# A third row tile for one key and one value tile, and a new timetable for the row work, in an attention block with norms and feed-forward on one Trainium2 core

## The chip, the cores and the metric

The kernel runs on one core of one Trainium2 chip. The metric is the device time of one execution in microseconds (us), the median of three runs. All arithmetic is in float32 apart from the stored mask.

## The reference

There are F = 8 graphs ("frames") of N = 2048 rows with C = 256 channels, H = 8 heads of D = 32, and one adjacency matrix for all of them. Cut to what matters:

```python
qkv = einsum('fnc,ck->fnk', x, w_qkv);  q, k, v = split(qkv, 3)      # heads of 32
scores = einsum('fnhd,fmhd->fhnm', q, k) / sqrt(32)
scores = where(adj > 0, scores, -1e9)
t = einsum('fhnm,fmhd->fnhd', softmax(scores), v)
a = layernorm(x + t) * ln1_g + ln1_b
h = relu(a @ w1 + b1)
b = layernorm(a + h @ w2 + b2) * ln2_g + ln2_b
out = layernorm(x + b)
```

So each row has one softmax attention over 2048 keys, then three norms: after the attention, after the feed-forward, and of the sum with x.

## The kernel before

**Items.** Rows go in chunks of 512 (`CH`), four of them a frame (`NCK`). The eight heads go in two groups `g` of four. Keys go in 16 blocks `mb` of 128. An item is (f, qc, g, mb): frame, chunk of query rows, group of heads, key block. There are 1024 items, 128 to a frame (`FRAME`), 32 to a chunk, and one pass of the main loop (one step) for each. A step `t` issues, in this order: side work (`advance(t)`), the exponentials of item t+1, the scores of item t+2, the values of item t, and the sums of item t.

- `scores` (L230, TensorE): four products key by query, one for each head, into two PSUM tiles of 128x1024. VectorE adds the mask on the way out into a `p` tile of 1 MB (L233, two adds).
- `exponentials` (L237, ScalarE): in place over the `p` tile.
- `values` (L249, TensorE): four products `p` by v, summed in PSUM over the 16 items of a group. At the last one ScalarE copies the sum to `oT` (L253).
- `add_up`: the denominators need the sum of the 16 `p` tiles of a group. Seven blocks (`POOLED` = 0, 3, 6, 8, 11, 13, 15) are added by GpSimd into block 0 (L271, `p<-p` of 128x2048). Eight others form two chains (`MOVED` = 1, 4, 7, 10 and 2, 5, 9, 12) that are summed by accumulating DMAs out of GpSimd's queue (L268, 1 MB each, also `p<-p`). Block 14 stays alone. Each transfer of a chain waits for the one before it.
- A generator `denominator` sums the four remaining tiles with a product by ones (L315); the last of the four terms is asked for four steps after the group's end (`SUM` = 4). ScalarE copies the result to `dT` (L317), TensorE transposes it, and VectorE takes the reciprocal and two running checks (L326 to L328).

There are 12 `p` tiles, which block t+2 takes in turn.

**A chunk's row work.** When both groups of a chunk have their denominators, `outcome` runs: `divide` transposes each `oT` and multiplies by the reciprocals (L353, VectorE) into a row tile `y`; a DMA out of GpSimd's queue adds x (L339, 512 KB). Then a generator `tail` does the rest:

- `norm`: statistics of four 128x256 blocks on VectorE (L278, L279), `per` blocks in a step; then four small GpSimd instructions (L283 to L287) that end in `nb`; after a pause, four ScalarE activations (L290).
- `feed_forward`: transposes into `turned` (L456, ScalarE copy L457), two GpSimd instructions over the row tile (L459, L461), the first product into `hT` (L54 with `w1s`, L470), and after a pause the second product (L54 with `w2s`), which VectorE adds to the row tile (L483).
- a second `norm`, two GpSimd instructions (L363, L365), a DMA out of GpSimd's queue that adds x again (L367), a pause, a third `norm`, and the store out of SP's queue (L370).

There are two `y` tiles, and `ROOM` lets two tails be open at once. The last chunk of all has a path of its own (`finish`, `half_rows`), in which two halves of the rows take turns.

**What sets the order.** [...] Side work sits in generators in a list with a first step and a due step each. At each step `advance` resumes those whose step has come; `yield n` means "go on n steps later", `yield BANK` asks for a PSUM bank, of which one new user is let in at a step, and `yield MORE` continues a product in parts. Side products are paid out of a credit of 2200 a step (`STEP`) against 2048 for a product of 512 columns, and a due generator may go on without credit. `TURNED`, `ROOM` and `INPUTS` hold a generator until a shared tile is free.

`NEXT` says at which step of a frame the next frame's work starts: `turn` (transposes of x, kept in DRAM as `xd`), `ask` (queries, `wqkv`) and `project` (keys and values of chunk c and group g, `wqkv`; reads its transposed rows back through SP's queue, L196, and copies the results with L189 and L215). The keys and values of a frame are 8 + 8 tiles; the pools `kp` and `vp` hold 11 each, so a frame's projections reuse tiles of the frame that is still running. SP's queue carries the masks (L151, eight a chunk), these reloads and the stores.

GpSimd's queue (POOL) carries in order: L271, the issue of L268, L339 and L367, the four instructions to `nb`, L363, L365, L459 and L461.

Of the kernel before, what the change touches and what calls it, by code (L numbers as in the profile page):

```python
# [29 lines left out]
BANK, MORE, WAIT, TURNED, ROOM, INPUTS = -1, -2, -3, -4, -5, -10  # L30
# [31 lines left out]
def fast_path(ctx, tc, cst, x, adj, out, RS):  # L62
    nc = tc.nc
    F, N, C = x.shape
    NCK, TPC, MB = N // CH, CH // P, N // P
# [2 lines left out]
    dp = ctx.enter_context(tc.tile_pool(name="dp", bufs=1, space=bass.MemoryType.DRAM))  # L68
    mkp = ctx.enter_context(tc.tile_pool(name="mkp", bufs=MB // 2 + 1))
    ld = ctx.enter_context(tc.tile_pool(name="ld", bufs=LD))  # L70
    kp = ctx.enter_context(tc.tile_pool(name="kp", bufs=3 * NCK - 1))
    qp = ctx.enter_context(tc.tile_pool(name="qp", bufs=4))
    vp = ctx.enter_context(tc.tile_pool(name="vp", bufs=3 * NCK - 1))
    pp = ctx.enter_context(tc.tile_pool(name="pp", bufs=12))
    work = ctx.enter_context(tc.tile_pool(name="work", bufs=1))
    yp = ctx.enter_context(tc.tile_pool(name="yp", bufs=2))
    op = ctx.enter_context(tc.tile_pool(name="op", bufs=1))
    small = ctx.enter_context(tc.tile_pool(name="small", bufs=4))

# [6 lines left out]
    state = {"pair": 0, "side": None, "turn": 0, "turned": False, "holder": None, "tails": 0, "credit": 0}  # L86

    def columns(out, lhsT, rhs, start, stop):
        state["credit"] -= 4 * out.shape[-1]
        in_columns(nc, out, lhsT, rhs, start, stop)  # L90

    def transposes(ps, src, ident=ident):
        state["credit"] -= TURN
        for j, s in enumerate(src):
            nc.tensor.transpose(ps[:, j * P:(j + 1) * P], s, ident)  # L95
# [178 lines left out]
    def norm(t, per=1):  # L274
        mv = small.tile([P, TPC, nc.vector.BN_AGGR_DIM], F32, name="mv")
        for j in range(TPC):
            st = small.tile([P, nc.vector.BN_STATS_DIM], F32, name="st")
            nc.vector.bn_stats(st, t[:, j, :])  # L278
            nc.vector.bn_aggr(mv[:, j, :], st)  # L279
            if j % per == per - 1:  # L280
                yield 1
        rs = small.tile([P, TPC], F32, name="rs")
        nc.gpsimd.tensor_scalar(rs, mv[:, :, 1], EPS, 1.0, op0=ALU.add, op1=ALU.mult)  # L283
        nc.gpsimd.tensor_tensor(rs, rs, cst["mhalf"], ALU.pow)  # L284
        nb = small.tile([P, TPC], F32, name="nb")
        nc.gpsimd.tensor_tensor(nb, mv[:, :, 0], rs, ALU.mult)
        nc.gpsimd.tensor_scalar(nb, nb, -1.0, 1.0, op0=ALU.mult, op1=ALU.mult)  # L287
        yield 2
        for j in range(TPC):
            nc.scalar.activation(t[:, j, :], t[:, j, :], AF.Identity, bias=nb[:, j:j + 1], scale=rs[:, j:j + 1])  # L290
            if j % per == per - 1:
                yield 1

    def rows(v):
        return v[:, None, :].to_broadcast([P, TPC, C])
# [37 lines left out]
    def outcome(f, qc):  # L333
        yield ROOM
        state["tails"] += 1
        xin = x[f, qc * CH:(qc + 1) * CH, :].rearrange("(p j) c -> p j c", p=P)
        y = yp.tile([P, TPC, C], F32, name="y")
        yield from divide(f, qc, y)
        nc.gpsimd.dma_start(y, xin, accum_op=ALU.add)  # L339
        begin = items.index((f, qc, 1, LAST)) + SUM + 2  # L340
        if (f, qc) == (F - 1, NCK - 2):
            start(begin + 5, tail(f, qc, y, xin, 2), begin + 8)
        else:
            start(begin + 10, tail(f, qc, y, xin), begin + 26)

    def divide(f, qc, y):
        rc = RC.pop((f, qc))
# [9 lines left out]
    def tail(f, qc, y, xin, per=1):  # L357
        yield from norm(y, per)
        yield from feed_forward(y)
        yield 1  # L360
        z = y
        yield from norm(z, per)
        nc.gpsimd.tensor_tensor(z, z, rows(cst["g2r"]), ALU.mult)  # L363
        yield 1
        nc.gpsimd.tensor_tensor(z, z, rows(cst["be2r"]), ALU.add)  # L365
        yield 1
        nc.gpsimd.dma_start(z, xin, accum_op=ALU.add)  # L367
        yield 7
        yield from norm(z, per)
        nc.sync.dma_start(out[f, qc * CH:(qc + 1) * CH, :].rearrange("(p j) c -> p j c", p=P), z)  # L370
        state["tails"] -= 1
# [65 lines left out]
    def finish(f, qc):  # L437
        y = yp.tile([P, TPC, C], F32, name="y")
        xr, xb = state["rows"]
        yield from divide(f, qc, y)  # L440
        yT, hT = (work.tile([P, 2, CH], F32, name=n) for n in ("turned", "hT"))
        dst = out[f, qc * CH:(qc + 1) * CH, :].rearrange("(p j) c -> p j c", p=P)
        both = [half_rows(h, y, xr, xb, yT, hT, dst) for h in range(2)]
        while both:
            for e in list(both):
                if next(e, both) is both:
                    both.remove(e)

    def feed_forward(y):
        yield TURNED  # L450
        state["turned"] = True
        yT = work.tile([P, 2, CH], F32, name="turned")
        for a in range(2):
            yield BANK
            ps = bank()
            transposes(ps, [y[:, j, a * P:(a + 1) * P] for j in range(TPC)])  # L456
            nc.scalar.activation(yT[:, a, :], ps, AF.Identity, bias=cst["be1c"][:, a:a + 1], scale=cst["g1c"][:, a:a + 1])  # L457
        yield 1
        nc.gpsimd.tensor_tensor(y, y, rows(cst["g1r"]), ALU.mult)  # L459
        yield 1  # L460
        nc.gpsimd.tensor_tensor(y, y, rows(cst["be1b2r"]), ALU.add)  # L461
        hT = work.tile([P, 2, CH], F32, name="hT")
        for d in range(2):
            yield BANK
            ps = bank()
            for a in range(2):
                if a:
                    yield MORE
                columns(ps, w1s[:, a, d * P:(d + 1) * P], yT[:, a, :], start=(a == 0), stop=(a == 1))
            nc.scalar.activation(hT[:, d, :], ps, AF.Relu, bias=cst["b1s"][:, d:d + 1], scale=1.0)  # L470
        state["turned"] = False
        yield 1
        z = y
        for jj in range(0, TPC, 2):
            yield BANK
            ps = bank()
            for j in range(jj, jj + 2):
                if j > jj:
                    yield MORE
                for d in range(2):  # L480
                    columns(ps[:, (j - jj) * C:(j - jj + 1) * C], hT[:, d, j * P:(j + 1) * P], w2s[:, d, :],
                            start=(d == 0), stop=(d == 1))
            nc.vector.tensor_tensor(z[:, jj:jj + 2, :], ps.rearrange("p (b c) -> p b c", c=C), z[:, jj:jj + 2, :], ALU.add)  # L483
# [4 lines left out]
    def start(t, gen, due):  # L488
        fill.append([t, gen, 1, due])
        fill.sort(key=lambda e: e[3])  # L490
# [13 lines left out]
    def advance(t, finish=False):  # L504
        state["credit"] = min(max(state["credit"], 0) + STEP, KEPT)
        state["now"] = t
        free = not state["holder"]

        def more():
            if state["holder"] and state["holder"][2] == WAIT:  # L510
                return False
            due = [e[3] for e in fill if e[2] == BANK and e[0] <= t or e is state["holder"]]
            return finish or state["credit"] >= UNIT or min(due) <= t

        if state["holder"]:
            resume(state["holder"], t)
            while state["holder"] and more():
                resume(state["holder"], t)
        inputs = True
        for e in list(fill):  # L520
            while e[2] is not None and e[0] <= t and e is not state["holder"]:
                if e[2] == BANK:
                    if not free or not more():
                        break
                    free = False
                elif e[2] < INPUTS:
                    inputs = inputs and not any(u is not None for u in live[:INPUTS - e[2]])
                    if not inputs:
                        break
                elif e[2] == TURNED and state["turned"] or e[2] == ROOM and state["tails"] == 2:  # L530
                    break
                resume(e, t)
            while e is state["holder"] and more():
                resume(e, t)
# [6 lines left out]
    def ask(f, c):  # L541
# [2 lines left out]
        give(xT)  # L544

    NEXT = {1: [(turn, 0)], 2: [(ask, 1)], 20: [(turn, 1)], 34: [(ask, 2)], 40: [(project, 0, 0)], 50: [(turn, 2)],
            60: [(project, 1, 0)], 66: [(ask, 3)], 72: [(turn, 3)], 80: [(project, 2, 0)], 98: [(ask, 0)], 100: [(project, 3, 0)],
            104: [(project, 0, 1)], 108: [(project, 1, 1)], 112: [(project, 2, 1)], 116: [(project, 3, 1)]}

    def begin():  # L550
        todo = deque((qc, c) for qc in range(NCK) for c in range(NCK))
# [319 lines left out]
```

## Time and profile before

| | before |
|---|---|
| median of 3 runs | 3245.36 us (3242.5 to 3246.28) |
| profiled execution: time / span | 3246.02 us / 3244.1 us |
| PE (TensorE matmul) busy | 3109.4 us, 96% |
| DVE (VectorE) busy | 2735.7 us, 84% |
| ACT (ScalarE) busy | 2435.8 us, 75% |
| POOL (GpSimd) busy | 2592.2 us, 80% |
| mean granted TensorE clock | 0.985 |
| DMA | 590.52 MB, mean 182 GB/s; GpSimd's own queue (software) 66.9% of 16 engines' span |

How to read it. The profile is of one execution; its span is the time from its first to its last instruction. Busy time is that of data instructions; a matmul's end is modelled, so 96% on PE does not say that PE ran at its peak. PEld is the weight load, which overlaps PE. A group line gives line, engine, operation, output<-input, tile shapes, how often, then busy time and mean ns of one, then the idle time of the engine ahead of these instructions and what ended most of it. A line for DMA issues gives output<-input, queue, count, KB each and the median us from issue to landing. In a timeline a line gives start (us), duration, engine, source line, operation, output<-input, and in brackets the wait before it and what ended it ("issue" where the profile shows no other cause). Line numbers are those of the kernel before.

### The profile page before, as it was taken

The page shows a single profiled execution, that of the slowest core. Times are in us where ns is not written, and L with a number is a line of the kernel's source. Part 1 is how long each engine was busy: PE and PEld are TensorE (multiplying, and loading weights), DVE is VectorE, ACT ScalarE, POOL GpSimd, SP SyncE. Part 2 cuts the span into 40 slices and gives each one's busy share as a digit, 9 for nine tenths or more (in the row PEclk, how much of TensorE's full clock was granted, in tenths as well). Part 3 has the DMA queues.
Part 4 walks back from the last instruction along what each step waited for, and adds up shares of the span by engine and source line. Part 5 has one row for each costly group of instructions (what it writes and reads, how often), then busy time and mean ns, then how long its engine had stood idle before and what let it go on. Part 6 is the DMA issues. An engine that isn't in the chain of part 4 may idle for free.

```text
span 3244.1 us, 68406 instructions
## 1 busy us (share of the span) xinstructions
PE 3109.4 (96%) x28996; PEld 979.0 (30%) x28996; DVE 2735.7 (84%) x3203; ACT 2435.8 (75%) x1941; POOL 2592.2 (80%) x1358
## 2 busy tenths in 40 slices
PE   7899999999999999999999999999999999998985
PEld 4222333223332233322233323323233323332222
DVE  4888888888888888888988888888888888888975
ACT  3667778777777777778777778777778777777774
POOL 0568888888878888788887888888888788878884
PEclk8899999999999999999999999999999999999998
DMA  9688779778879788788787879878788878877763
GB/s 320 145 181 185 183 176 199 178 177 196 181 176 207 171 188 193 159 195 200 178 181 174 185 174 221 177 167 198 173 192 197 177 168 198 181 171 161 166 145 86
DMA packets 153240, 590.52 MB, mean 182 GB/s; under 512 B 15040, under 2 KB 67776, under 8 KB 103904
## 3 DMA queue, kind: packets, MB, share of 16 engines
q0 software_dynamic: 64416, 434.80, 66.9%
q1 hardware_dynamic: 87696, 149.98, 13.1%
q8 instruction: 229, 3.75, 0.4%
q10 hardware_dynamic: 816, 1.31, 0.1%
q14 instruction: 83, 0.68, 0.1%
HBM read 146.67 MB, written 37.75 MB: 57 GB/s over the span
## 4 chain that ended last, share of the span: by engine, by line
PE 75%; DVE 7%; POOL 5%; issue 4%; DMA 4%; ACT 2%; DVEq 0%; POOLq 0%; ACTq 0%
PE s L230 27%; PE x L249 24%; PE x L54 14%; PE x L315 6%; DVE p L233 6%; PE x L95 4%; DMA p<-p 3%; POOL p L271 2%; ACT p L237 1%; DMA mask<-md 1%; POOL y L365 1%; DVE st L278 1%; POOL y L363 0%; POOL y L461 0%; POOL y L459 0%
## 5 line engine op out<-in xcount | busy, mean ns | idle before, releaser
L233 DVE TENSOR_TENSOR p<-s,mask 128x1024 f32<-128x1024 f32 x2048 | 2409.3, 1218 | 372.7 <-PE s L230 209.9
L237 ACT ACTIVATE p<-p 128x2048 f32<-128x2048 f32 x1024 | 1956.1, 1910 | 521.4 <-DVE p L233 465.6
L271 POOL TENSOR_TENSOR p<-p 128x2048 f32<-128x2048 f32 x381 | 1825.5, 4793 | 223.7 <-ACT p L237 221.3
L230 PE MATMUL s<-qT,kT 32*128 32x512 f32 x8192 | 1173.8, 643 | 40.8 <-DVE p L233 35.9
L249 PE MATMUL x<-p,v 128*32 128x512 f32 x8192 | 1096.0, 607 | 16.7 <-ACT p L237 16.4
L268 POOL DMA_DIRECT2D p<-p x383 | 359.3, 956 | 306.9 <-ACT p L237 88.3
L230 PEld LDWEIGHTS s<-qT,kT 32*128 32x128 f32 x8192 | 321.1, 183 | 644.7 <-DVE p L233 587.2
L249 PEld LDWEIGHTS x<-p,v 128*32 128x32 f32 x8192 | 161.6, 108 | 797.8 <-issue 310.6
L315 PE MATMUL x<-p,ones 128*32 128x512 f32 x2080 | 268.2, 594 | 17.9 <-POOL p L271 11.1
L290 ACT ACTIVATE y<-y,nb,rs 128x256 f32<-128x256 f32 x372 | 218.7, 590 | 40.4 <-POOL nb L287 40.4
L54 PE MATMUL x<-in,wqkv 128*32 128x512 f32 x1888 | 243.5, 592 | 0.0
L278 DVE BATCH_NORM_STATS2 st<-y 128x6 f32<-128x256 f32 x372 | 154.9, 416 | 5.1 <-DMA y<-in_x_dram 5.1
L54 PE MATMUL x<-turned,w1s 128*32 128x512 f32 x992 | 123.5, 596 | 0.4 <-ACT in L166 0.4
L54 PE MATMUL x<-w2s,hT 128*32 128x256 f32 x2016 | 121.8, 382 | 2.1 <-DVE y L483 2.1
L54 PEld LDWEIGHTS x<-wqkv,in 128*32 128x32 f32 x3584 | 102.2, 110 | 63.4 <-issue 58.9
L315 PEld LDWEIGHTS x<-p,ones 128*32 128x32 f32 x2080 | 66.3, 110 | 178.2 <-issue 140.4
L54 PE MATMUL x<-wqkv,in 128*32 128x128 f32 x3584 | 117.3, 273 | 0.0
L54 PEld LDWEIGHTS x<-in,wqkv 128*32 128x32 f32 x1888 | 61.7, 110 | 140.9 <-issue 113.7
L284 POOL TENSOR_TENSOR rs<-rs,mhalf 128x4 f32<-128x4 f32 x93 | 96.3, 1036 | 7.8
L54 PEld LDWEIGHTS x<-w2s,hT 128*32 128x32 f32 x2016 | 65.4, 111 | 75.0 <-issue 33.0
L363 POOL TENSOR_TENSOR y<-y,g2r 128x1024 f32<-128x1024 f32 x31 | 82.5, 2663 | 5.3 <-ACT y L290 5.3
L461 POOL TENSOR_TENSOR y<-y,be1b2r 128x1024 f32<-128x1024 f32 x31 | 83.0, 2679 | 0.6
(116 smaller groups left out, 1335.7 us busy)
## 6 DMA issues: line engine op xcount, KB each, us to landing
p<-p POOLq DMA_DIRECT2D x383, 1024.0 KB, 10.4
in<-xd SPq DMA_DIRECT2D x87, 512.0 KB, 10.6
mask<-md SPq DMA_DIRECT2D x248, 128.0 KB, 7.9
y<-in_x_dram POOLq DMA_DIRECT2D x62, 512.0 KB, 8.1
p<-in_adj_dram SPq DMA_DIRECT2D x16, 1024.0 KB, 10.7
out_dram<-y SPq DMA_DIRECT2D x31, 512.0 KB, 6.2
in<-in_x_dram SPq DMA_DIRECT2D x29, 512.0 KB, 15.5
xd<-in SPq DMA_DIRECT2D x28, 512.0 KB, 11.2
```

The costliest lines, as they stand in the source:

```text
L54: nc.tensor.matmul(out[r:r + D], lhsT[:, r:r + D], rhs, start=start, stop=stop)
L95: nc.tensor.transpose(ps[:, j * P:(j + 1) * P], s, ident)
L230: nc.tensor.matmul(ps2[half][:, j, :], KT[f, mb // TPC, g][r:r + D, (mb % TPC) * P:(mb % TPC + 1) * P], QT[f, qc, g][r:r + D, :], start=Tr ...
L233: nc.vector.tensor_tensor(pt[:, 2 * half:2 * half + 2, :], ps, MK[f, qc, mb // 2][:, mb % 2, None, :].to_broadcast([P, 2, CH]), ALU.add)
L237: nc.scalar.activation(PT[item], PT[item], AF.Exp, scale=1.0 / math.sqrt(D))
L249: nc.tensor.matmul(O[grp][r:r + D, :], V[f, mb // TPC, g][:, mb % TPC, r:r + D], PT[item][:, h, :], start=(mb == 0), stop=(mb == LAST))
L268: nc.gpsimd.dma_start(PT[f, qc, g, chain[0]], PT.pop(item), accum_op=ALU.add)
L271: nc.gpsimd.tensor_tensor(first, first, PT.pop(item), ALU.add)
L278: nc.vector.bn_stats(st, t[:, j, :])
L284: nc.gpsimd.tensor_tensor(rs, rs, cst["mhalf"], ALU.pow)
L290: nc.scalar.activation(t[:, j, :], t[:, j, :], AF.Identity, bias=nb[:, j:j + 1], scale=rs[:, j:j + 1])
L315: nc.tensor.matmul(ps[r:r + D, :], cst["ones"], term[:, h, :], start=(n == 0), stop=(n == len(blocks) - 1))
```

## The change

Four things change together.

1. **Memory.** `kp` and `vp` go from 11 to 10 tiles each, `yp` from 2 to 3, and `ROOM` from two open tails to three.
2. **Projections.** In `NEXT` the last two of group 0 and the four of group 1 start at steps 100, 104, 108, 112, 116 and 120 of a frame instead of 80, 100, 104, 108, 112 and 116.
3. **Tail.** A tail starts one step later (begin + 11, due begin + 28, instead of 10 and 26). Between the issue of `nb` and L290 there are four steps instead of two where one block of statistics goes in a step, three where two go. The second product of the feed-forward comes three steps after the first one's last part instead of one. The pause ahead of the third norm is nine steps instead of seven (eight with two blocks in a step).
4. **End.** In the last frame every tail takes two blocks a step and starts at begin + 9, due begin + 12; before, only the chunk before the last did, at begin + 5 and begin + 8. In `finish` a pass over the two halves gives way once to other side work.

```diff
-    kp = ctx.enter_context(tc.tile_pool(name="kp", bufs=3 * NCK - 1))
+    kp = ctx.enter_context(tc.tile_pool(name="kp", bufs=3 * NCK - 2))
-    vp = ctx.enter_context(tc.tile_pool(name="vp", bufs=3 * NCK - 1))
+    vp = ctx.enter_context(tc.tile_pool(name="vp", bufs=3 * NCK - 2))
-    yp = ctx.enter_context(tc.tile_pool(name="yp", bufs=2))
+    yp = ctx.enter_context(tc.tile_pool(name="yp", bufs=3))
...
     def norm(t, per=1):
...
-        yield 2
+        yield max(5 - per, 2)
...
     def outcome(f, qc):
...
-        if (f, qc) == (F - 1, NCK - 2):
-            start(begin + 5, tail(f, qc, y, xin, 2), begin + 8)
+        if f == F - 1:
+            start(begin + 9, tail(f, qc, y, xin, 2), begin + 12)
         else:
-            start(begin + 10, tail(f, qc, y, xin), begin + 26)
+            start(begin + 11, tail(f, qc, y, xin), begin + 28)
...
     def tail(f, qc, y, xin, per=1):
...
         nc.gpsimd.dma_start(z, xin, accum_op=ALU.add)
-        yield 7
+        yield 10 - per
         yield from norm(z, per)
...
     def finish(f, qc):
...
                 if next(e, both) is both:
                     both.remove(e)
+            yield 1
...
     def feed_forward(y):
...
         state["turned"] = False
-        yield 1
+        yield 3
...
-                elif e[2] == TURNED and state["turned"] or e[2] == ROOM and state["tails"] == 2:
+                elif e[2] == TURNED and state["turned"] or e[2] == ROOM and state["tails"] == 3:
...
     NEXT = {1: [(turn, 0)], 2: [(ask, 1)], 20: [(turn, 1)], 34: [(ask, 2)], 40: [(project, 0, 0)], 50: [(turn, 2)],
-            60: [(project, 1, 0)], 66: [(ask, 3)], 72: [(turn, 3)], 80: [(project, 2, 0)], 98: [(ask, 0)], 100: [(project, 3, 0)],
-            104: [(project, 0, 1)], 108: [(project, 1, 1)], 112: [(project, 2, 1)], 116: [(project, 3, 1)]}
+            60: [(project, 1, 0)], 66: [(ask, 3)], 72: [(turn, 3)], 98: [(ask, 0)], 100: [(project, 2, 0)],
+            104: [(project, 3, 0)], 108: [(project, 0, 1)], 112: [(project, 1, 1)], 116: [(project, 2, 1)], 120: [(project, 3, 1)]}
```

## The prediction

> **What bounds the kernel now.** The page first:
>
> ```profile
> PE 3109.4 (96%) x28996; PEld 979.0 (30%) x28996; DVE 2735.7 (84%) x3203; ACT 2435.8 (75%) x1941; POOL 2592.2 (80%) x1358
> L233 DVE TENSOR_TENSOR p<-s,mask 128x1024 f32<-128x1024 f32 x2048 | 2409.3, 1218 | 372.7 <-PE s L230 209.9
> L271 POOL TENSOR_TENSOR p<-p 128x2048 f32<-128x2048 f32 x381 | 1825.5, 4793 | 223.7 <-ACT p L237 221.3
> p<-p POOLq DMA_DIRECT2D x383, 1024.0 KB, 10.4
> ```
>
> Four engines are nearly full, so a share says little; I read steps instead. One step is one item (f, qc, g, mb), from one value product (L249) to the next; 1024 steps make 3.1 of the 3.24 ms. Taken from the starts of L249 in the timeline, a step costs 2.93 us with one 512-column side product, 2.65 to 2.75 with four transposes, 3.78 with two side products, 3.79 with one L483 product, 2.56 with none. Those prices over all steps give 3027 us; the rest, 64 us, is waiting, in some 60 steps. The waits view names it:
>
> ```profile
> POOL p L268 <- DMA p<-p: 75.5, 32, 5.5
> ACT y L290 <- POOL nb L287: 40.4, 16, 6.9
> PEld x L315 <- POOL p L271: 18.6, 13, 3.0
> DVE y L483 <- POOL y L461: 9.5, 6, 2.1
> ```
>
> Each line: who waited for whom, us, times, longest. All of it starts at POOL, whose queue is strictly in order. Its timeline in frame 4, steps 562 to 577, shows how:
>
> ```profile
> 1788.63 0.89 POOL L367 DMA_DIRECT2D y<-in_x_dram  x1 [0.30 <-POOL y L365]
> ...
> 1803.40 0.87 POOL L268 DMA_DIRECT2D p<-p  x1
> 1804.33 4.58 POOL L271 TENSOR_TENSOR p<-p 128x2048 f32<-128x2048 f32 x1
> 1808.90 0.89 POOL L268 DMA_DIRECT2D p<-p  x1
> 1817.05 0.86 POOL L268 DMA_DIRECT2D p<-p  x1 [7.26 <-issue]
> ```
>
> The p<-p transfer of 1803.40 landed 13.1 us later; the next of its chain (L268 at 1817.05) waits for that landing, and POOL stands 7.26 us. Everything behind it is late: the nb of a norm, so ACT stands at L290, the exponentials behind it are late and PE loses 1.9 us.
>
> VectorE has almost no slack in a transpose step:
>
> ```profile
> 1762.31 0.68 DVE L353 TENSOR_TENSOR y<-x,rc 128x512 f32<-128x512 f32 x1
> 1762.90 2.34 DVE L233 TENSOR_TENSOR p<-s,mask 128x1024 f32<-128x1024 f32 x2
> 1765.17 0.68 DVE L353 TENSOR_TENSOR y<-x,rc 128x512 f32<-128x512 f32 x1
> 1765.76 2.34 DVE L233 TENSOR_TENSOR p<-s,mask 128x1024 f32<-128x1024 f32 x2
> ```
>
> Start to start, two mask adds take 2.27 us and L353 0.59: 2.86 in a step for which PE needs 2.75, and those steps do take 2.86. One block of statistics (L278, L279) adds 0.56, the three L326 to L328 together 0.24. So VectorE is the bound wherever its sum exceeds PE's price, after about 0.3 us of lead.
>
> **The change, part by part**, with the order of both programs' instructions at hand. Sums are made against the profiled execution, 3246.0 us (span 3244.1); the runs' median is 3245.4, so no correction.
>
> *Projections four steps later, second product two steps later: PE.* No work is added or removed. Double steps go from 68 to 91, empty ones from 61 to 82. A double and an empty step cost 3.78 + 2.56 where two single ones cost 5.85: 0.49 more, times 21: **+10 us**. The moved projections' L196 loads pass SP's mask loads (L151); a mask is needed some 30 steps later, so I take nothing; a late one would cost up to its 7.9 us landing.
>
> *One key and one value tile fewer.* A copy into a kT or v might wait for the last product of the old one. The rows show no such wait now; below, the order puts a release before each reuse (0), above, one step for each of 7 frames (20). I take 0: nothing in L189's row points to it.
>
> *Statistics on other steps: VectorE.* With the second product and the first norm later, the second norm's four L278 land on dT, oT, oT and the step after, four times in a frame (521, 553, 584, 616 in frame 4 are the first oT steps). VectorE then needs 2.27+0.56+0.24, twice 2.27+0.59+0.56, and 2.27+0.56: 3.07 + 2 x 3.42 + 2.83 = 12.74 us, where PE needs 2.75+2.75+2.75 and 2.65 or 2.93: 10.9 to 11.2. Less 0.3 of lead, 1.3 to 1.5 us four times a frame, 5.7, where the same count for the order of before gives 0.8. 4.9 times six frames and 2 in the first: **+32 us**.
>
> *Last frame, two blocks per step.* All its tails now take two statistics per step (3.39 us of VectorE), on steps where PE has nothing (2.56), and twice two tails coincide: four blocks, 4.5 us, in each of steps 975 and 1007. Counted step by step, with two L290 and the `turned` copy on one ACT step (981, 1013): **+11 us**.
>
> *Longer waits: stalls that go.* nb gets four steps instead of two (11.7 us for 5.9), which covers the 6.9 us worst wait. The stalls found in the step distances: 21 us at L290, 3 at L483, 18 at L315 in step (f,2,1,4), where L363, L365 and L367 stood before the last POOLED add and now come after it. In the last frame the statistics no longer wait for a transfer just issued:
>
> ```profile
> 3128.36 0.43 DVE L278 BATCH_NORM_STATS2 st<-y 128x6 f32<-128x256 f32 x1 [5.13 <-DMA y<-in_x_dram]
> ```
>
> That is 7 us beyond what VectorE's own work takes there. A few tenths of waits stay. **-44 us** (6.7 in the first frame, on a p<-p landing, remain).
>
> *What is late next.* The same moves carry L363, L365 and the DMA of L367 into the middle of a group. In the POOL timeline above L367 (1788.63) stands ahead of the group's six p<-p transfers; changed, it stands between the second and the third (step 566, mb 6), with 5 us of adds. These transfers pass one after another: L268 of 1765.18 landed after 7.9 us, L339 of 1766.14 after 11.6, L268 of 1766.70 after 16.5, that is at 1773.1, 1777.7, 1783.2: 512 KB hold the queue 4.6 us, 1 MB 5.5. POOL from exp(563) at 1790.0: L271 4.6, L363 2.4, nb 1.7, L268 0.9, L365 2.6, L268 0.6, L367 0.9, L271 4.6 brings the third transfer to 1808.1 instead of 1803.4. It lands near 1823.9 (the same 13.1 us, plus what is left of L367 in front), so the next L268 goes at 1824 instead of 1817, and the rest (L271, L268 after another landing at 1829, L271, L459, L461, L271) ends at 1844. PE asks for that last add in step 580, now at about 1839 because its own ACT stall is gone: **a stall of 5 us at (f,2,0,4)**. The same count one tile later, at (f,3,0,4): last add ready 27.3 us after exp(604), asked for at 23.5: **3.8 us**. Bounds for each: 0, if the transfers overlap fully, and 7.3, the whole wait of before again. I take 8.8 a frame, seven frames, and 8 for two such places in the last: **+70 us**.
>
> The skill has a rule for this price: "DMA: Bandwidth & Descriptors", section "Anatomy of one DMA", gives about 2.0 us fixed plus bytes over 436 GB/s. By it L367 would hold the queue 1.2 us instead of 4.6, both stalls would shrink by some 3.4, and the total would be near 3276. The landings above disagree with it (6.9 us was the shortest for 1 MB, the rule says 4.4), and the trace decides.
>
> After the 3.0 us wait at (2,2,1,4) the granted clock in 1112 to 1117 is 0.66 and the next step costs 0.8 more; after the two-part wait at 1888 to 1892 it stays 1.00. Up to 14 times 0.8, 11 us, belongs to the upper end.
>
> A page speaks against long new waits: "TensorE: Matmul & The Clock Gate", Part 1, puts the array at half rate after an idle window of about 3.4 us. By it each 5 us stall would bring about 1.7 us more, 24 in all; this trace shows it after some waits only.
>
> *Tail.* The last L363 and L365 (2.4 us each) now stand among the last chunk's POOL steps; two of those move by 0.9: **+1 us**.
>
> Sum: 3246 + 10 + 32 + 11 - 44 + 70 + 1 = **3326 us**.
>
> **The rivals.** (A) The forecast, new POOL stalls included: 3290 to 3375. (B) They are hidden: without the 70 it is 3256, with a third of it 3279; still slower. For it: L271 of mb 15 had 4 us to spare at 1939. Against: POOL already stands 75.5 us for p<-p landings. (C) Faster: VectorE's added statistics slip into time in which it waits for PE (209.9 us in all at L233), and POOL's stalls go: 3246 + 10 + 1 - 44 = 3213 with neither 32 nor 11 nor 70. It decides if VectorE's excess and new stalls together stay under 33 us. Against: the 2.86 us steps show VectorE setting the pace with 0.1 us excess. (D) Worse: 12 p buffers, mostly reused 9 items later; a POOL lag of 14 us plus a 10 us landing exceeds the 19 us this leaves, so L233 waits too: another 20 to 50, 3346 to 3376 and above. (E) The third y tile might never be used; but the order shows a tail ending 66 steps after its start with two begun since, so it is.
>
> **How the numbers follow.** A 0.60, B 0.19, C 0.12, D 0.09: C gets more than its row speaks for, since the 32 and the 70 are both counted by hand. Point: A's, 3326. The range takes most of A, nearly all of B and the nearer part of D: 3262 to 3372, leaving out C, B's lowest edge and D's upper part, about 2 in 10. About 0.2% (6.5 us) is what a measurement tells from no change. Faster: C less its near edge, 0.10; same: the edges of B and C, 0.05; slower: 0.85.
>
> **What would show it.** Right: step distances of 3.4 us at the second oT step and the one after, four times a frame; L290 hardly waiting for L287; the L315 row waiting more for L271 and p<-p, at (f,2,0,4) and (f,3,0,4); L268's own wait for p<-p above 75.5; two-block steps of 3.4 us in the last frame. Wrong: L315's wait falling, or transpose steps with statistics at 2.75. If L233 waits on p<-p or L271, D has joined in.

## The result, and the profile after

The changed kernel takes 3390.29 us (median of 4 runs, 3389.82 to 3397.54) beside 3243.93 us for the kernel before in the same comparison: a ratio of 1.0457, 95% interval 1.0439 to 1.0475, so 146 us slower. The forecast was 3326 us in a range of 3262 to 3372. The sign was right and most of the named mechanisms were there; the size was short by 64 us, and the time lies 18 us above the range. The profiled execution took 3390.07 us, span 3388.3.

The distances from one L249 to the next place the loss:

| | before, us | after, us |
|---|---|---|
| until the first L249 | 98.9 | 97.5 |
| frame 0 | 370.0 | 380.9 |
| frames 1 to 6, each | 384.1 to 391.0 | 409.0 to 410.3 |
| frame 7 | 397.3 | 401.6 |
| after the last L249 | 47.6 | 50.7 |

So 127 of the 144 us between the two profiled executions are lost in frames 1 to 6, some 21 us in each. The page after, for the lines shown of before:

```profile
PE 3148.3 (93%) x28996; PEld 983.4 (29%) x28996; DVE 2740.0 (81%) x3203; ACT 2439.2 (72%) x1941; POOL 2596.1 (77%) x1358
L233 DVE TENSOR_TENSOR p<-s,mask 128x1024 f32<-128x1024 f32 x2048 | 2410.3, 1219 | 530.1 <-PE s L230 287.5
p<-p POOLq DMA_DIRECT2D x383, 1024.0 KB, 11.8
in<-in_x_dram SPq DMA_DIRECT2D x29, 512.0 KB, 17.4
```

The last of these lines in the kernel before:

```profile
in<-in_x_dram SPq DMA_DIRECT2D x29, 512.0 KB, 15.5
```

The work is the same to 5 us on VectorE, ScalarE and GpSimd; transfers land 1.4 us (chains) and 1.9 us (loads of x) later. The waits view after (who waited for whom, us, times, longest):

```profile
POOL p L268 <- DMA p<-p: 158.3, 52, 8.0
DVE p L233 <- DMA p<-p: 78.4, 44, 5.1
PE x L95 <- DMA in<-in_x_dram: 37.3, 6, 7.4
PEld x L315 <- DMA p<-p: 28.5, 15, 5.1
ACT y L290 <- POOL nb L287: 6.0, 3, 3.0
```

L268's own wait has doubled (75.5 before), L290's is nearly gone (40.4 before), and two rows are new: VectorE waits for chain transfers before it can write a `p` tile (1.7 us before, once), and TensorE waits six times, 6 us each, for a load of x (no such row before). That second one is neither in the forecast's sum nor in a rival. TensorE's timeline in frame 4, step 574, item (4,1,1,14):

```profile
1902.06 1.06 PE L249 MATMUL x<-p,v 128*32 128x512 f32 x8
1910.06 1.08 PE L95 MATMUL x<-ident,in 128*128 128x128 f32 x4 [6.94 <-DMA in<-in_x_dram]
```

L95 here is the transpose of the third 512 rows of x for the next frame. The load (L172) was issued at 1885.20 and landed after 24.7 us. In frame 4 of the kernel before the same load, which landed after 20.1 us, had 56 us until its transposes:

```profile
1802.80 1.19 SPq L172 DMA_DIRECT2D in<-in_x_dram  x1
1859.25 0.66 PE L95 MATMUL x<-ident,in 128*128 128x128 f32 x4
```

VectorE on an oT step of the kernel after (a step that transposes an `oT`), as forecast:

```profile
1839.62 0.42 DVE L278 BATCH_NORM_STATS2 st<-y 128x6 f32<-128x256 f32 x1
1840.08 0.18 DVE L279 BATCH_NORM_AGGREGATE mv<-st 128x2 f32<-128x6 f32 x1
1840.17 0.66 DVE L353 TENSOR_TENSOR y<-x,rc 128x512 f32<-128x512 f32 x1
1840.75 2.35 DVE L233 TENSOR_TENSOR p<-s,mask 128x1024 f32<-128x1024 f32 x2
```

The four instructions fill 3.39 us from one L278 to the next, and that step and the one behind it take 3.39 us. GpSimd's timeline in the group (4,2,1):

```profile
1987.23 0.93 POOL L268 DMA_DIRECT2D p<-p  x1 [0.31 <-issue]
1987.88 1.18 POOL L367 DMA_DIRECT2D y<-in_x_dram  x1
...
2011.01 0.85 POOL L268 DMA_DIRECT2D p<-p  x1 [5.39 <-DMA p<-p]
...
2017.96 0.87 POOL L268 DMA_DIRECT2D p<-p  x1 [1.51 <-ACT p L237]
```

The first transfer shown (mb 4) goes 6.5 us after the end of its exponentials, the last, the group's sixth (mb 12), 14.6 us after. What comes of it, VectorE at step 610, item (4,3,0,2):

```profile
2017.63 2.36 DVE L233 TENSOR_TENSOR p<-s,mask 128x1024 f32<-128x1024 f32 x2 [1.26 <-DMA p<-p]
...
2024.89 2.36 DVE L233 TENSOR_TENSOR p<-s,mask 128x1024 f32<-128x1024 f32 x2 [4.36 <-DMA p<-p]
```

L233 waits until the transfer of 2011.01, 13.8 us on its way, has let go of the tile that item 612 is to have.

### The profile page after: what moved, and what is told of

Its sections match the earlier page's. It is cut to its first block, busy times and chain, and to the rows that moved or that the text cites. A ratio compares the mean times of both kernels' runs of the same rounds, so it can differ in the third digit from the quotient of the medians.

```text
span 3388.3 us, 68329 instructions
## 1 busy us (share of the span) xinstructions
PE 3148.3 (93%) x28996; PEld 983.4 (29%) x28996; DVE 2740.0 (81%) x3203; ACT 2439.2 (72%) x1941; POOL 2596.1 (77%) x1358
## 4 chain that ended last, share of the span: by engine, by line
PE 57%; DMA 21%; DVE 11%; POOL 3%; issue 3%; ACT 2%; SPq 0%; POOLq 0%; DVEq 0%; ACTq 0%
PE s L230 21%; PE x L249 17%; DMA p<-p 16%; PE x L54 11%; DVE p L233 8%; PE x L315 6%; DMA in<-in_x_dram 4%; POOL p L271 2%; PE x L95 2%; ACT p L237 1%; DVE st L278 1%; DVE y L353 1%; DMA y<-in_x_dram 0%; ACT y L290 0%; DVE mv L279 0%
## 5 line engine op out<-in xcount | busy, mean ns | idle before, releaser
L233 DVE TENSOR_TENSOR p<-s,mask 128x1024 f32<-128x1024 f32 x2048 | 2410.3, 1219 | 530.1 <-PE s L230 287.5
L271 POOL TENSOR_TENSOR p<-p 128x2048 f32<-128x2048 f32 x381 | 1842.8, 4837 | 179.1 <-ACT p L237 175.7
L249 PE MATMUL x<-p,v 128*32 128x512 f32 x8192 | 1104.3, 611 | 1.3 <-ACT p L237 1.1
L268 POOL DMA_DIRECT2D p<-p x383 | 382.0, 1027 | 479.0 <-DMA p<-p 158.3
L249 PEld LDWEIGHTS x<-p,v 128*32 128x32 f32 x8192 | 162.0, 108 | 790.3 <-issue 335.8
L315 PE MATMUL x<-p,ones 128*32 128x512 f32 x2080 | 273.1, 608 | 19.4 <-DMA p<-p 17.0
L54 PE MATMUL x<-in,wqkv 128*32 128x512 f32 x1888 | 244.8, 593 | 1.9
L290 ACT ACTIVATE y<-y,nb,rs 128x256 f32<-128x256 f32 x372 | 217.7, 591 | 6.0 <-POOL nb L287 6.0
L278 DVE BATCH_NORM_STATS2 st<-y 128x6 f32<-128x256 f32 x372 | 154.8, 416 | 1.9 <-DMA y<-in_x_dram 1.9
L315 PEld LDWEIGHTS x<-p,ones 128*32 128x32 f32 x2080 | 67.3, 112 | 184.7 <-issue 140.8
L54 PE MATMUL x<-w2s,hT 128*32 128x256 f32 x2016 | 120.7, 380 | 0.0
L54 PE MATMUL x<-turned,w1s 128*32 128x512 f32 x992 | 120.6, 593 | 0.0
L54 PEld LDWEIGHTS x<-wqkv,in 128*32 128x32 f32 x3584 | 102.2, 110 | 62.9 <-issue 52.4
L54 PE MATMUL x<-wqkv,in 128*32 128x128 f32 x3584 | 117.1, 273 | 0.0
L54 PEld LDWEIGHTS x<-in,wqkv 128*32 128x32 f32 x1888 | 59.7, 110 | 148.1 <-issue 120.4
L317 ACT COPY dT<-x 128x512 f32<-128x512 f32 x64 | 37.4, 585 | 84.2 <-PE x L315 84.2
L363 POOL TENSOR_TENSOR y<-y,g2r 128x1024 f32<-128x1024 f32 x31 | 74.2, 2393 | 25.0 <-ACT y L290 24.9
L54 PEld LDWEIGHTS x<-w2s,hT 128*32 128x32 f32 x2016 | 65.4, 110 | 70.2 <-issue 37.2
## 6 DMA issues: line engine op xcount, KB each, us to landing
p<-p POOLq DMA_DIRECT2D x383, 1024.0 KB, 11.8
in<-xd SPq DMA_DIRECT2D x87, 512.0 KB, 11.8
y<-in_x_dram POOLq DMA_DIRECT2D x62, 512.0 KB, 10.6
```

Of the source, the lines that this page charges most:

```text
L54: nc.tensor.matmul(out[r:r + D], lhsT[:, r:r + D], rhs, start=start, stop=stop)
L233: nc.vector.tensor_tensor(pt[:, 2 * half:2 * half + 2, :], ps, MK[f, qc, mb // 2][:, mb % 2, None, :].to_broadcast([P, 2, CH]), ALU.add)
L249: nc.tensor.matmul(O[grp][r:r + D, :], V[f, mb // TPC, g][:, mb % TPC, r:r + D], PT[item][:, h, :], start=(mb == 0), stop=(mb == LAST))
L268: nc.gpsimd.dma_start(PT[f, qc, g, chain[0]], PT.pop(item), accum_op=ALU.add)
L271: nc.gpsimd.tensor_tensor(first, first, PT.pop(item), ALU.add)
L315: nc.tensor.matmul(ps[r:r + D, :], cst["ones"], term[:, h, :], start=(n == 0), stop=(n == len(blocks) - 1))
```

## The experiments

All times are medians; the ratio is to the kernel before, measured beside each. "After" and "before" in the second column say which kernel the edit is made to.

| run | edit | us | ratio to before (95%) |
|---|---|---|---|
| changed kernel | | 3390.3 | 1.0457 (1.0439 to 1.0475) |
| e1 | after: transposes of x later | 3347.1 | 1.0319 (1.0300 to 1.0338) |
| e2 | after: one block of statistics | 3394.6 | 1.0479 (1.0458 to 1.0501) |
| e3 | after: no L367 | 3323.8 | 1.0251 (1.0228 to 1.0274) |
| e4 | after: old tail times | 3257.0 | 1.0048 (1.0031 to 1.0065) |
| e5 | after: old norm wait | 3396.2 | 1.0471 (1.0454 to 1.0489) |
| e6 | after: old product wait | 3316.5 | 1.0225 (1.0196 to 1.0254) |
| e7 | after: L367 late | 3410.5 | 1.0519 (1.0501 to 1.0536) |
| e8 | before: third norm waits | 3227.5 | 0.9956 (0.9939 to 0.9972) |
| e9 | projections and memory alone | 3238.8 | 0.9985 (0.9975 to 0.9994) |
| e10 | e5 with the third norm's long wait | 3364.6 | 1.0363 (1.0346 to 1.0380) |
| e11 | e3 and e2 together | 3303.0 | 1.0179 (1.0158 to 1.0201) |
| e12 | before: no L367 | 3235.5 | 0.9971 (0.9961 to 0.9981) |
| e13 | e10 without L363, L365 | 3286.3 | 1.0123 (1.0107 to 1.0140) |
| e14 | after: no L363, L365 | 3326.1 | 1.0243 (1.0226 to 1.0261) |
| e15 | e8 and e9 together | 3224.1 | 0.9932 (0.9915 to 0.9949) |

"Excess" below is what steps take beyond the prediction's prices, put down to the longest wait in the step.

**e1, the load of x.**

```diff
 def turn(f, c):
-        yield 5
+        yield 9
         yield from turn_rows(xc, xT)
```

> The kernel after, with one number changed: the generator that loads 512 rows of x and transposes them waits 9 steps between load and transposes instead of 5. In a frame this moves the transposes of the third load from step 62 back to step 74, 18 steps after the load, where the kernel before has them. Theory: the 46 us that TensorE loses at (f,1,1,14) in frames 1 to 6, waiting for that load (25 us from issue to landing), is a term of its own, and goes: about 3345 us, and no wait of L95 for the load. Rival: the 8 us pause lets GpSimd's queue and the transfers of the chains catch up, and without it the stall of 4 to 5 us that the prediction put at (f,2,0,4) appears in its place: a gain of 46 less 18 to 28, so 3362 to 3372 us.

43 us less: the theory's number. The excess at L95, 45.7 us, is 0. The rival is right about one thing: the stall that the prediction put at (f,2,0,4) comes up, as waits of L233 for p<-p at (f,2,0,2), 2.3 to 4.4 us in frames 1 to 4 and 6. The waits view of this run has

```profile
DVE p L233 <- DMA p<-p: 91.3, 43, 5.9
```

against 78.4, but L315's row for p<-p falls from 28.5 to 19.6, so little comes back in all.

**e2, VectorE's statistics.** In the second norm, L278 for the first block only.

```diff
+            if j < own:            # own = 1 in the second norm
+                one = st
                 nc.vector.bn_stats(st, t[:, j, :])
-            nc.vector.bn_aggr(mv[:, j, :], st)
+            nc.vector.bn_aggr(mv[:, j, :], one)
```

> The kernel after, with the statistics of the second norm taken of the first block only (three of four L278 left out; the aggregation L279 stays, on the first block's numbers), so VectorE has 3 x 0.45 us less work for each tail and nothing else moves. Theory: VectorE is the bound on the transpose steps of oT; they fall from 3.39 to about 2.95 us and the run by 25 to 36 us, to 3354 to 3365 us. Rival: those steps are long for another reason (ScalarE, or products that wait for banks): under 8 us gained, 3382 us or more.

Nothing gained (the intervals overlap), yet not for the rival's reason. VectorE's timeline in this run (its L281 is L279, its L355 is L353):

```profile
1836.38 0.17 DVE L281 BATCH_NORM_AGGREGATE mv<-st 128x2 f32<-128x6 f32 x1
1836.47 0.65 DVE L355 TENSOR_TENSOR y<-x,rc 128x512 f32<-128x512 f32 x1
1837.04 2.34 DVE L233 TENSOR_TENSOR p<-s,mask 128x1024 f32<-128x1024 f32 x2
1839.31 0.17 DVE L281 BATCH_NORM_AGGREGATE mv<-st 128x2 f32<-128x6 f32 x1
```

The step is 2.93 us instead of 3.39, and the excess of these steps fell from 41 to 14. What was gained was lost again in waits for transfers:

```profile
PEld x L54 <- DMA in<-xd: 18.3, 6, 3.5
```

Chain waits of L233 and of the products by ones took 10 us more, and products that wait for a reload (L54 for in<-xd) 14 us that were not there. This fits that VectorE's long steps had been giving the transfers time; e11 puts that to the test.

**e3, e12 and e11, the transfer of L367.** e3 and e12 leave out the second accumulation of x, in the kernel after and in the kernel before; e11 is e3 with e2's edit.

```diff
-        nc.gpsimd.dma_start(z, xin, accum_op=ALU.add)     # L367
         yield 10 - per
```

> The kernel after without the DMA of L367 (the second accumulation of x, 512 KB, is left out; the third norm then runs on the row tile alone). Theory: this transfer in the middle of a group's chains is what makes the third and fourth chain transfers late; waits of L233 and L315 for p<-p fall by half or more, and the run by 35 to 70 us, to 3320 to 3355 us. Rival: the two GpSimd instructions over the row tile (L363, L365, 5 us together) ahead of the third transfer do it, and the DMA hardly counts: under 15 us gained, 3375 us or more.

> The kernel before without the DMA of L367 (the second accumulation of x left out). Theory: there it is issued at mb 14 to mb 1, between the chains of two groups, and costs under 12 us: 3230 to 3243 us, against 66 us in the kernel after. Rival: its bytes cost the same wherever they are: 3190 us or less.

> The kernel after without the DMA of L367 (the second accumulation of x left out) and with the second norm's statistics of the first block only. Alone, the first edit gave 66 us and the second nothing. Theory: VectorE's long steps gave the late chains time, so their removal was taken back by waits for p<-p; with the transfer out, the chains have room and 20 to 28 us of VectorE's excess go on top: 3296 to 3304 us. Rival: the chains and GpSimd's adds set the pace even so: 3315 us or more.

66 us, 9 us and, with the statistics, another 21 us, each inside the theory's range. The same 31 transfers cost 2.1 us each in the kernel after and 0.3 us each in the kernel before. The waits of e3:

```profile
DVE p L233 <- DMA p<-p: 40.6, 16, 5.5
...
PE x L95 <- DMA in<-in_x_dram: 4.4, 5, 1.4
```

L233's row has halved, and the wait for the load of x is nearly gone though it is asked for at the same step: it lands after 18.2 to 19.2 us in frames 1 to 6 instead of 21.8 to 25.2. That matters for the 66 us: the excess at L95 falls from 45.7 to under 6, so some 40 of them are the load's wait, and some 26 are left for the chains. And the stall that the prediction named comes up where it named it, at (f,2,0,4), 1.7 to 4.8 us in seven frames, as L315 waiting for L271, here in frame 4:

```profile
1885.73 0.16 PEld L315 LDWEIGHTS x<-p,ones 128*32 128x32 f32 x8 [3.61 <-POOL p L271]
```

Once the chains have room, VectorE's term counts (e11), as it did not in e2.

**e4 and e9, the parts of the change.** e4 puts back the four numbers of the tail's timetable; e9 also the last frame.

```diff
-        yield max(5 - per, 2)
+        yield 2
-            start(begin + 11, tail(f, qc, y, xin), begin + 28)
+            start(begin + 10, tail(f, qc, y, xin), begin + 26)
-        yield 10 - per
+        yield 7
-        yield 3                    # ahead of the second product
+        yield 1
```

> The kernel after with the timetable of the tail as in the kernel before (start at begin + 10, due begin + 26; two steps from nb to L290; one step ahead of the second product; seven ahead of the third norm), and with the memory, the projections and the last frame as changed. Theory: the tail's timetable carries nearly all of the loss; what stays is 9 us of step prices, 12 us of the last frame, less some 8 us of waits that the last frame loses: 3250 to 3265 us. Rival: the moved projections or the third row tile carry a good part of it: 3290 us or more.

> The kernel after with the tail's timetable and the last frame as in the kernel before: what is left of the change is the memory (10 key and value tiles, three row tiles), the projections four steps later and the extra turn in the finish. Theory: the 14 us that the run with the old tail times lay above the kernel before are the last frame's two blocks a step; this one is within 6 us of the kernel before, 3237 to 3249 us. Rival: they are the projections and the memory: 3251 to 3258 us.

Both inside the theory's range: the timetable of the tail carries 133 us, the last frame's edits some 18 by the medians (in the profiled executions 6 in frame 7 and 8 behind the last step), and the later projections (four steps, one of them twenty) with one key and one value tile less cost nothing; e9 is even 6 us below the kernel before. In e4 GpSimd's wait for p<-p (L268) is below that of before again: 66.0 us beside 75.5.

**e5, e6 and e10, one wait at a time.** e5 undoes only the norm's wait (`yield max(5 - per, 2)` back to `yield 2`), e6 only the product's (`yield 3` back to `yield 1`); e10 is e5 with the long wait kept in the third norm.

> The kernel after with one of its waits undone: two steps from nb to L290 in every norm, as before (the wait ahead of the second product stays at three steps). L367 then stands at mb 2 to 4 of the group g = 1 instead of mb 5 to 6, so ahead of the first or second chain transfer, and the transposes of the third load go to step 74; the second norm's statistics stay on the oT steps, and nb is waited for again. Theory (place of L363 to L367 in the chains): the load's 46 us go, the waits for p<-p more than halve, 10 to 20 us at L290 come back, VectorE's 41 us stay: 3290 to 3325 us. Rival (the wait for the product does it, this one nothing but the load): 3345 us or more, as with the later transposes alone.

> The kernel after with the other wait undone: the second product one step after the first one's last part, as before (four steps from nb to L290 stay). L367 then stands at mb 2 to 3 of g = 1, ahead of all or all but one of the group's chain transfers, the second norm's statistics fall on steps 4 to 8 of a chunk, off the oT steps, and the third load is still transposed 6 steps after its issue. Theory: VectorE's 41 us fall under 12, the waits for p<-p more than halve, and the load lands some 5 us sooner with no transfer put between the chain's, so its wait falls under 20 in all: 3250 to 3285 us. Rival (the load is late for its own reason): its 46 us stay, 3290 to 3320 us.

> As the run with the old norm wait (two steps from nb to L290), but the third norm keeps the long wait (four steps). The place of L363 to L367 stays ahead of the chains. Theory: the 120 us at L290 in that run were third norms whose nb stood behind the late adds at the end of a chain; two steps more (5.9 us) cover all but some 25 us of them, the waits for p<-p stay under 20 us and the load's at nothing: 3290 to 3320 us. Rival: GpSimd is late there whatever waits for it, and the time comes back at L315 and L233: 3350 us or more.

e5 missed: its time lies in the rival's range, though not for the rival's reason. The load's 46 us did go and the chain waits fell from 72 to 14 us of excess, as expected, but the waits for nb gave 120 us, not 10 to 20:

```profile
ACT y L290 <- POOL nb L287: 168.3, 36, 9.4
```

They are third norms, at (f,3,0,2 to 3), (f,0,0,2) and (f,2,0,4): their nb stands behind the last adds of a group, which run some 10 us late. e10 gives those norms two steps more, and the rival wins: L290's excess falls to 15 us, and 61 us come up at L315 for L271 in the same groups. So GpSimd is late at the end of a group whoever waits for it. e6's time lies in the rival's range, its rows between the two: VectorE's excess fell to 12, about as the theory said, and the load's to 23, halfway. What the theory did not have are waits of L233 for p<-p at (f,0,0,8), 28 us in frames 2 to 7.

**e7, L367 alone moved behind the chain.**

```diff
-        yield 1
+        yield 1 if per == 2 else 9
         nc.gpsimd.dma_start(z, xin, accum_op=ALU.add)
-        yield 10 - per
+        yield 10 - per if per == 2 else 5
```

> The kernel after with L367 alone moved: issued nine steps after L365 instead of one (mb 13 to 14 of g = 1, after the last chain transfer), the third norm five steps after it; not in the last frame. The bytes are the same and L363 and L365 stay where they are. Theory (its place between the chain's transfers costs the time): close to the run without this transfer, 3315 to 3345 us, with the third load's wait under 15 us in all. Rival (what counts is the number of bytes that share the transfer engines, wherever they are): 3370 us or more.

A miss by its own doing: five steps were too few for the third norm.

```profile
DVE st L278 <- DMA y<-in_x_dram: 90.7, 20, 7.4
```

The load's excess fell to 8 and the chain waits (L233 and L315 for p<-p) from 72 to 34, which speaks for the place; 74 us of excess came up at L278 and 28 at L315 for L271. The time is in the rival's range, but with these waits of its own the run does not decide between the two.

**e13 and e14, GpSimd's two instructions over the row tile.** L363 and L365 left out, ahead of the chains (e13, from e10) and in their middle (e14, from the kernel after).

```diff
-        nc.gpsimd.tensor_tensor(z, z, rows(cst["g2r"]), ALU.mult)
         yield 1
-        nc.gpsimd.tensor_tensor(z, z, rows(cst["be2r"]), ALU.add)
         yield 1
         nc.gpsimd.dma_start(z, xin, accum_op=ALU.add)
```

> As the run in which the norms wait two steps and the third norm four (L363 to L367 at mb 0 to 4, ahead of the chains), without L363 and L365 (the scaling by ln2_g and the addition of ln2_b are left out); the DMA of L367 stays. Theory: GpSimd's 4.8 us at mb 0 to 3 make the first chain transfer late, and three landings one after another carry that to the group's end; without them the waits of L315 for L271 (61 us) fall under 20: 3300 to 3330 us. Rival: landings alone set the end of the chain, GpSimd's work ahead of them hardly counts: 3350 us or more.

> The kernel after without L363 and L365 (the scaling by ln2_g and the addition of ln2_b left out); the DMA of L367 stays where it is. Theory: GpSimd's 4.8 us ahead of the third chain transfer cost about as much as the transfer of L367 (66 us): 3315 to 3355 us. Rival: only the transfer does: 3375 us or more.

78 and 64 us, e13 even 14 us below its theory's range: 4.8 us of GpSimd per tail, on an engine with 23% of its time idle, cost as much as the transfer. In e14 the load's wait stays (the row of L95 is 35.8 beside 37.3), so its 64 us are nearly all in waits for the chains. In e13 the row of L315 for L271 went to

```profile
PEld x L315 <- POOL p L271: 25.8, 26, 3.7
```

from 54.5 in e10. How it happens is seen in the mean delay from an item's exponentials to GpSimd's add or transfer, over the groups g = 1 of frames 1 to 6 (us):

| | mb 4 | mb 5 | mb 7 | mb 10 | mb 12 | mb 15 |
|---|---|---|---|---|---|---|
| before | 4.7 | 1.9 | 3.3 | 7.3 | 9.4 | 6.8 |
| after | 6.5 | 5.0 | 6.2 | 12.2 | 12.4 | 10.6 |
| e3 (no L367) | 6.7 | 5.6 | 6.4 | 10.2 | 10.8 | 10.6 |
| e14 (no L363, L365) | 4.1 | 2.1 | 3.7 | 10.1 | 9.9 | 8.3 |
| e10 | 6.9 | 4.4 | 5.9 | 8.7 | 9.7 | 9.5 |
| e13 | 4.3 | 1.9 | 3.5 | 7.1 | 8.1 | 7.9 |

Work on GpSimd at mb 0 to 6 delays the second transfer by 3 us; each chain then passes three landings one after another (medians of 8 to 14 us in the kernel after), so the delay is still there at mb 15. L367 adds to the landings. In the kernel before the same work is issued at mb 12 to mb 1, where only the last adds of the group and the first of the next one are behind it.

**e8 and e15, better than both.** e8 gives the third norm of the kernel before four steps from nb to L290 and starts the tail of the chunk before the last at begin + 7; e15 adds e9's memory and projections.

```diff
-    def norm(t, per=1):
+    def norm(t, per=1, wait=2):
...
-        yield 2
+        yield wait
...
-        yield from norm(z, per)    # the third
+        yield from norm(z, per, 4)
```

> The kernel before with two waits longer and nothing else: four steps instead of two from nb to L290 in the third norm only (behind it stands nothing but the store), and the tail of the chunk before the last starts at begin + 7 instead of begin + 5. Theory: the waits at L290 for nb (18 us on the path) go without any GpSimd or VectorE work moving, and 4 of 7 us of the wait of L278 in the last frame: 3215 to 3230 us, faster than the kernel before. Rival: the time comes back as waits at L315 or L233 for the chains, as ScalarE no longer holds the steps back: 3238 to 3248 us.

> The kernel after's memory, projections and finish, the tail's timetable of before, four steps from nb to L290 in the third norm only, and the tail of the chunk before the last from begin + 7. Theory: the 6 us of the run with the projections alone and the 15 us of the run with the longer third norm add up: 3218 to 3227 us. Rival: they do not add up: 3228 us or more.

Both came in as expected: 15 and 22 us faster than the kernel before, ratios 0.9956 and 0.9932. e8 holds two edits, which no run takes apart; frames 1 to 6, where only the third norm's wait differs, are 13.5 us shorter together. In e8 the row for nb is down from 40.4 to

```profile
ACT y L290 <- POOL nb L287: 7.2, 3, 3.6
```

What the change wanted from its longer norm wait was to be had where nothing stands behind the wait but the store.

## Why the prediction missed

The terms of its sum beside the excess in the trace after, less that before. A step is put down whole to one wait, so the split is good to some 8 us; the load's row does not depend on it:

| term | forecast, us | trace, us |
|---|---|---|
| step prices | +10 | +9.1 |
| VectorE on transpose steps | +32 | +40.5 |
| last frame | +11 | +11.8 |
| stalls that go (L290, L315 for L271, L278, L483) | -44 | -34.4 |
| new stalls by L363, L365, L367 | +70 | +61.7 |
| a load of x that is late | none | +45.7 |
| steps beside a wait, other | none | +8.1 |
| outside the steps | +1 | +1.7 |

**The step that failed is one that was never taken.** The prediction's sum has no term for the loads of x and so took them at nothing, without a reason; what they cost was 45.7 us. It followed what the change delays, and did not ask what moves up into the slots that are left. With four steps from nb to L290 the first feed-forward product leaves step 62 of a frame, and `turn`, which had waited for a free bank since step 61, takes it: transposes six steps (asked for 18 us) after the load, where before they came 18 steps after. Both numbers to see it were in the profile of before: `turn` waits five steps, under 15 us, and loads of x have a median of 15.5 us to landing, 19 to 26 us at this place. e1 shows it as 43 us by itself. Without it the kernel is at 3347 us, inside the range and 21 above the point.

**The 70 us were right in sum, wrong in place.** They were put at L315 in (f,2,0,4) and (f,3,0,4). In the trace they are waits of L233 for a `p` tile at (f,3,0,2), 2.9 to 5.3 us in seven frames, and at (f,0,1,2), 1.4 to 2.6 us in six, and of L315 at (f,1,1,2 to 3). At (f,2,0,4) there is nothing: TensorE has just stood 5.5 to 8.8 us at (f,1,1,14). Without that pause the wait is there, two steps sooner in e1 and at the very place in e3. That the sum came out near 62 is therefore partly luck. Rival D named this way in (a chain that is late when its tile is taken again nine items later); it is not on top of A but the form that A took. The measured time lies above D's 3376, but the load took it there, which D does not have. The cause behind the 70 was half of the truth: the forecast priced L367's time in the transfers' queue (4.6 us) and GpSimd's 5 us together; e3 and e14 show 66 and 64 us for the one and the other. Of the 66 some 40 are the load's wait, which L367 makes longer; the 64 are nearly all in the chains, as much as the new stalls together. So the two costs do not add up.

**VectorE's 32 us were there in the steps, and nothing in the total**, as long as the chains were late (e2), and 21 us when they had room (e11). On the dT and oT steps and the one behind them alone, the excess goes from 4.6 us before to 37.3 after, the forecast's figure; the rest of the row's 40.5 is in other steps. A sum of terms is not what leaving out a term returns. **The stalls that go** were 34, not 44; where the other 10 us are was not traced. **The step prices** came out as forecast, but not from the projections: with these alone (e9) the prices of the steps add up to 1 us more than before, so the rest is the tail's. One sum is short: 3027 and 64 us make 3091, the steps of the trace 3097.6; the 6.7 us of the first frame, which the prediction names later, are missing there.

**The clock.** The forecast kept a slower clock after new stalls in the upper end only. The mean granted clock went from 0.985 to 0.975. Windows of the kernel after (us, length, busy of PE, PEld, DVE, ACT, POOL, granted clock, DMA share, GB/s) around the 8 us wait:

```profile
1902.00:1909.90 7.90, 1.13 (x12) 0.16 (x8) 2.35 (x2) 1.91 (x1) 7.17 (x4) 0.88 1.06 280
1909.90:1913.00 3.10, 2.94 (x12) 1.23 (x12) 0.00 (x0) 1.81 (x2) 3.10 (x1) 0.50 1.04 221
1913.00:1916.00 3.00, 3.00 (x24) 0.77 (x24) 2.69 (x3) 0.85 (x2) 2.92 (x3) 0.71 1.04 224
1916.00:1919.00 3.00, 3.00 (x28) 0.79 (x28) 2.15 (x3) 2.42 (x3) 3.00 (x2) 1.00 0.81 170
```

Half the clock for the 3 us behind the wait, and the step behind it 0.4 to 1.0 us longer; behind the waits at (f,3,0,2) the granted clock is 0.50 again (2024 to 2030 us), and in five frames the next step is 1.6 to 1.8 us longer with no wait in it that the profile shows. That belongs in the sum, some 2 us a frame. The page "TensorE: Matmul & The Clock Gate", Part 1, of the Trainium skill (half rate after an idle window of about 3.4 us) fits these rows, where TensorE had stood 6.9 and 4.3 us. It does not cover the kernel before at (2,2,1,4): TensorE's wait there was 2.0 us by its row, and the granted clock was still 0.66 from 1112 to 1117.

**A rule weighed again.** The load of x of 512 KB lands in 4.8 us at the first step, in 24.7 us in the kernel after and in 19.2 us without L367 (frame 4). The Trainium skill's "DMA: Bandwidth & Descriptors", section "Queues, rings and completion order", says that each transfer engine takes turns between the queues that have work, so a load out of SP's queue should get slower with more traffic in GpSimd's: these three rows agree. The fit that the same page gives comes to an estimate of 1.2 us for the bytes of L367; that is under the 2.1 us per transfer of e3 and above the 0.3 us of e12, so the bytes alone do not set what a transfer costs here; what stands behind it differs between the two.

**Left open.** Why L363 and L365 cost more ahead of the chains (78 us) than in their middle (64), and why e9 is 6 us below the kernel before (43 us instead of 48 behind the last step, but 51 in e4 with the same `finish`), was not tried. That L367 behind the chains would be harmless in the new timetable is argued from e3, e7 and e12, not shown.

## What to carry to other kernels

When an edit delays work in an order that the program writes out, list also what moves up into the slots it leaves, and set each such step's distance from its load against the landing time in the trace. Keep work off the queue that issues a serial chain of transfers until the chain's last issue is out: ahead of it the delay was carried through the landings to the consumer (e13, e14). That the work is free behind the chain no run of the new timetable shows; in the old one, where it stands there, L367 cost 9 us. Lengthen a wait where nothing hangs on it: two steps more in the third norm gained 13.5 us in frames 1 to 6 (e8), the timetable that has them in every norm, with its other new times, lost 133.

## What the runs showed of the hardware that was not expected

The time to land a 512 KB load went from 4.8 us to 25 us with the traffic around it, and leaving out L367, one other 512 KB transfer for each row tile, brought the load to 19. GpSimd is idle for 23% of the span in the kernel after and the packets of its queue take 64% of the time of 16 engines, and yet in three pairs of runs (the kernel after with e3 and with e14, e10 with e13) one 512 KB transfer, or two GpSimd instructions of 2.4 us, cost 2.1 to 2.5 us of the total for each row tile, where they stand in front of or inside a chain; in e3 mostly by way of the load of x.
